# Attention scores as two half-width products of TensorE each, in place of one full-width product

## The chip, the core and the metric

The kernel runs on one core of a Trainium2 chip. The engines of the core that matter here are TensorE (PE in the profile; its weight loads are listed apart, as PEld), VectorE (DVE), ScalarE (ACT), GpSimd (POOL) and SyncE (SP), which issues most of the DMAs. The metric is the device time of one execution, in microseconds; lower is better. All values are fp32.

## The reference

The program is a "macaron" layer on x of 8 batches x 1024 tokens x 256 features: half a mixture-of-experts feed-forward, a causal attention, and another half feed-forward, each on the layer-normed x and added to it. Cut to what matters:

```
x = x + 0.5 * ffn(layernorm(x))
x = x + attn(layernorm(x))
x = x + 0.5 * ffn(layernorm(x))

attn:  q, k, v = projections, 16 heads of 16 features
       dots = (q * 16**-0.5) @ k.T          # 1024 x 1024 for each batch and head
       dots = where(j > i, -1e9, dots)      # causal
       out  = softmax(dots) @ v;  return out @ Wo.T + bo
ffn:   top-2 routing over 8 experts; an expert's tokens count only if they
       are at most 1280 (counts <= cap), otherwise the whole expert is left out
```

With these inputs every expert is asked for more than its capacity, so both feed-forwards add nothing. The kernel computes the routing counts and branches over the feed-forward; the trace shows no load of expert weights. What runs is the attention and the routing.

## The kernel before, in words

The attention works in 32 units: 8 batches x 4 groups of 4 heads (`u`, `b`, `g`). For a unit, qT and kT hold its 4 heads on 128 partitions, 32 for each head: 16 features, and one row that carries a correction. On the key side that row is -1, on the query side it is first 0 and later the row maximum, so that the second score product comes out with its maximum already subtracted.

Each head's scores are computed twice. `m_steps` (`block`, L862) computes them with queries on the partitions (tiles named sm): VectorE takes the row maximum from them, with the causal mask added on the diagonal block. `settle` (L893) carries the maxima through DRAM into qT. `e_steps` (`scores`, L910) computes them with keys on the partitions (tiles named sc): ScalarE writes their exponential to pT in SBUF, GpSimd zeroes the upper triangle of the diagonal block, and `values` (L934) multiplies pT by v (tile pav), with a column of ones beside v that gives the row sums.

A score product has 32 rows of contraction (a head's partitions), 128 stationary columns and 128 to 512 moving columns. The head decides the 32 partitions, and so the row group of the 128 x 128 array; four heads use the four row groups. The other large products (pav; pv, pq and px, the projections) go through `matmul_cols` (L714): 128 rows of contraction by 32 stationary columns, four of them on the four column groups.

A unit has 24 steps. In the main loop (L1241) a step issues, for h = 0 and 1, one sc product of unit u and one sm product of unit u + 1: four products on four row groups, in the order sc, sm, sc, sm. After them come the pav products of an earlier step (two steps later for the first half of the columns, three for the second), and a piece of other work (`Beside.step`, L79: projections of coming units, layer norms, output projection, routing). The wrapper `InOrder` (L27) keeps the instructions of TensorE, VectorE, ScalarE and GpSimd in the order written.

Score products write to six PSUM banks that are handed out in turn (`score`, L695); the other two banks (`bank`, L699) serve everything else. A step asks for four score banks, so its first two products use those of the second head of two steps before, and its last two those of the first head of the step before. A bank is free once ScalarE (sc) or VectorE (sm) has read it.

Of the kernel before, what the change touches and what calls it, by code (L numbers as in the profile page):

```python
# [18 lines left out]
P = 128  # L19
# [81 lines left out]
def macaron_kernel(  # L101
# [78 lines left out]
    for k in range(4):  # L180
        gpsimd.affine_select(
            out=row16,
# [498 lines left out]
    def attention(run_no, src, dst, gate0, logits, tally):  # L681
# [3 lines left out]
        with stack:  # L685
# [9 lines left out]
            def score(name):  # L695
                asked[0] += 1
                return ps_score.tile([P, 512], F32, tag=f"score{asked[0] % 6}", name=name)

            def bank(name):  # L699
                return ps_bank.tile([P, 512], F32, tag="bank", name=name)  # L700
# [5 lines left out]
            def matmul(out, lhsT, rhs, start=True, stop=True):  # L706
                pe.matmul(out, lhsT=lhsT, rhs=rhs, start=start, stop=stop)
# [6 lines left out]
            def matmul_cols(out, lhsT, rhs, start=True, stop=True):  # L714
                for r in range(0, P, 32):
                    matmul(out[r : r + 32], lhsT[:, r : r + 32], rhs, start, stop)

            xbs, xnTs, lns, stds, att_ds, gate_lns, lgs = {}, {}, {}, {}, {}, {}, {}


# [138 lines left out]
            def m_steps(u):  # L859
                qT, kT = qTs[u % 4], kTs[u % 4]  # L860

                def block(ib, j0, pr, h):  # L862
                    hf, i = divmod(ib, 4)
                    w = min(512, (ib + 1) * P - j0)
                    r = 64 * pr + 32 * h
                    sc = score(f"sm{u}_{ib}_{pr}_{j0}_{h}")
                    matmul(sc[:, :w], qT[r : r + 32, ib * P : (ib + 1) * P], kT[r : r + 32, j0 : j0 + w])
                    if j0 + w < (ib + 1) * P:
                        so_far = first[ib, r] = ap.tile([P, 1], F32, tag="first", name=f"first{u}_{ib}_{r}", bufs=18)
                        vector.tensor_reduce(so_far, sc[:, :w], AX.X, ALU.max)  # L870
                    else:

                        vector.tensor_tensor_reduce(
                            out=sc[:, :w],
                            in0=sc[:, :w],
                            in1=causal[:, 512 - w :],
                            scale=1.0,
                            scalar=first.pop((ib, r), LOWEST),
                            op0=ALU.add,
                            op1=ALU.max,  # L880
                            accum_out=tops[hf][:, r // 8 + i : r // 8 + i + 1],
                        )

                first = {}
                todo = [(ib, 0) for ib in (3, 2, 1, 0)]
                todo += [(ib, 0) for ib in (4, 5, 6, 7)] + [(ib, 512) for ib in (7, 6, 5, 4)]
                for ib, j0 in todo:
                    for pr in range(2):
                        yield lambda h, ib=ib, j0=j0, pr=pr: block(ib, j0, pr, h)
# [15 lines left out]
            def e_steps(u):  # L905
                b, g = divmod(u, NG)
                qT, kT = qTs[u % 4], kTs[u % 4]
                pav = {}

                def scores(hf, jb, pr, out, h):  # L910
                    off = max(0, jb - 4 * hf) * P
                    w = 512 - off
                    r = 64 * pr + 32 * h
                    sc = score(f"sc{u}_{hf}_{jb}_{pr}_{h}")
                    matmul(sc[:, :w], kT[r : r + 32, jb * P : (jb + 1) * P], qT[r : r + 32, hf * 512 + off : hf * 512 + 512])
                    if h == 0:
                        out[pr] = ap.tile([P, 2, 512], F32, tag="pT", name=f"pT{u}_{hf}_{jb}_{pr}", bufs=8)
                    pT = out[pr]
                    scalar.activation(pT[:, h, :w], sc[:, :w], AF.Exp)
                    if h == 0:  # L920
                        return
                    if jb >= 4 * hf:
                        gpsimd.affine_select(
                            out=pT[:, :, :P],
                            in_=pT[:, :, :P],
                            pattern=[[0, 2], [1, P]],
                            compare_op=ALU.is_ge,
                            fill=0.0,
                            base=0,
                            channel_multiplier=-1,  # L930
                        )


                def values(hf, jb, pTs, part):  # L934
                    if jb == 0 and part == 0:
                        pav[hf] = bank(f"pav{u}_{hf}")
                    off = max(0, jb - 4 * hf) * P
                    w = 512 - off
                    if w <= 256:
                        cols = slice(0, w)  # L940
                        if part == 1:
                            return
                    else:
                        cols = slice(part * w // 2, (part + 1) * w // 2)
                    for pr in (1, 0):
                        for h in range(2):
                            r = 64 * pr + 32 * h
                            v0 = (4 * g + 2 * pr + h) * VW
                            matmul(
                                pav[hf][r : r + 32, off + cols.start : off + cols.stop],  # L950
                                vaugs[b % 2][:, jb, v0 : v0 + 32],
                                pTs[pr][:, h, cols],
                                start=(jb == 0 and part == 0),
                                stop=(jb == 4 * hf + 3),
                            )
                    if u == NU - 1 and jb == 4 * hf + 3:
                        if part == 0:
                            last.append(pav.pop(hf))
                    elif jb == 4 * hf + 3 and part == 0:
                        att = ap.tile([P, 512], F32, tag="att", name=f"att{u}_{hf}", bufs=4)  # L960
                        scalar.copy(att, pav.pop(hf))
                        if g == 0:
                            att_ds[b, hf] = spill.tile(
                                [NH, 32, 512], F32, tag="att_d", name=f"att_d{run_no}_{b}_{hf}", bufs=3
                            )
                        nc.sync.dma_start(
                            out=att_ds[b, hf][4 * g : 4 * g + 4].rearrange("h r c -> (h r) c"), in_=att
                        )

                for hf in range(2):  # L970
                    for jb in range(4 * hf + 4):
                        pTs = {}
                        yield (lambda h, hf=hf, jb=jb, pTs=pTs: scores(hf, jb, 1, pTs, h)), None
                        yield (
                            (lambda h, hf=hf, jb=jb, pTs=pTs: scores(hf, jb, 0, pTs, h)),
                            (lambda part, hf=hf, jb=jb, pTs=pTs: values(hf, jb, pTs, part)),
                        )
# [319 lines left out]
    logits = [route.tile([P, NT, E], F32, name=f"logits{k}") for k in range(2)]  # L1297
    tallies = [tally_tile("0"), tally_tile("1")]
    leasts = attention(0, x, out, (logits[0], tallies[0]), logits[1], tallies[1])
    some0 = kept("0", leasts[0])  # L1300
    either = route.tile([P, 1], I32, name="either")
    vector.scalar_tensor_tensor(either, leasts[1], float(CAP), some0, ALU.is_le, ALU.max)
    with tc.If(branch_on(either) > 0):
        some1 = kept("1", leasts[1])

        with tc.If(flag(some0, "0") > 0):
            feed_forward(0, logits[0], x, xw_d)
            tally = tally_tile("1b")
            anew = attention(1, xw_d, out, None, logits[1], tally)
            vector.tensor_copy(some1, kept("1b", anew[1]))  # L1310
        with tc.If(flag(some1, "1") > 0):
            feed_forward(1, logits[1], out, out)
# [40 lines left out]
```

## Time and profile before

| what | value |
|---|---|
| time before, median of 3 runs | 1412.6 us (1409.44 to 1412.75) |
| the profiled execution: its time, its span | 1412.56 us, 1410.7 us |
| PE busy, share of the span | 1373.3 us, 97% |
| PE weight loads busy | 526.3 us, 37% |
| DVE, ACT, POOL busy | 73%, 56%, 28% |
| mean granted TensorE clock | 0.983 |
| sm product records | x3072, 537 ns in the mean |
| sc product records | x3072, 534 ns in the mean |
| pav product records | x5120, 370 ns in the mean |

An fp32 product stands in the profile as two records of a weight load (LDWEIGHTS) and two of a product (MATMUL), so 3072 records are 1536 products of the program. A form such as `32*128 32x512` reads: 32 active rows by 128 active columns of the array, moving operand 32 partitions x 512 columns. Records of TensorE overlap and their ends are modelled, so differences of starts tell more than durations. Nearly every operation of the attention is issued from one helper line (L37), so the names of the tiles tell the instructions apart. `x8` on a timeline row is a run of eight merged records. The busy time counts an engine as busy as long as any record of it is open.

### The profile page before, as it was taken

Reading aid. Unit: us, or ns where it says so; the run is one execution under the profiler, and the core shown is the slowest. Engines: PE = TensorE matmul, PEld = TensorE weight load, DVE = VectorE, ACT = ScalarE, POOL = GpSimd, SP = SyncE. Lnnn points to the kernel's source line nnn. Section 1 sums busy time; section 2 is a strip of 40 time slices with the busy share of each in tenths; the row PEclk is TensorE's granted clock in tenths of the full one; section 3 lists DMA queues with packets and bytes.
Section 4 is the critical chain, followed back from the end, with each engine's and each line's share of the span. In section 5 each row is a group of like instructions: output and inputs, shape, how many; then the busy total and the mean of one; then the engine's idle time right before and its main releaser. Section 6 shows DMA issues by size and latency. Waiting matters only on the chain.

```text
span 1410.7 us, 37948 instructions
## 1 busy us (share of the span) xinstructions
PE 1373.3 (97%) x14520; PEld 526.3 (37%) x14520; DVE 1032.9 (73%) x3417; ACT 788.5 (56%) x1790; POOL 399.0 (28%) x720
## 2 busy tenths in 40 slices
PE   7999999999999999999999999999999999999994
PEld 3334333343433333343333433334333333334431
DVE  4757677876778868777677777787677786778854
ACT  3246555555655656555555556555665565655561
POOL 3015114241143412352131421424114331222221
PEclk9889999999999999999999999999999999999997
DMA  4010101212111210212112121122111111121100
GB/s 146 10 40 26 41 25 50 57 61 72 34 54 60 73 44 29 78 49 71 40 35 70 43 87 32 48 65 69 52 32 58 55 47 41 42 65 63 42 26 33
DMA packets 66966, 72.85 MB, mean 52 GB/s; under 512 B 24688, under 2 KB 42232, under 8 KB 66776
## 3 DMA queue, kind: packets, MB, share of 16 engines
q1 hardware_dynamic: 65688, 69.82, 16.4%
q8 instruction: 116, 1.90, 0.5%
q14 instruction: 74, 0.61, 0.1%
q10 hardware_dynamic: 1088, 0.53, 0.1%
HBM read 26.87 MB, written 26.20 MB: 38 GB/s over the span
## 4 chain that ended last, share of the span: by engine, by line
PE 93%; DVE 3%; POOL 2%; issue 1%; DMA 0%; ACT 0%; ACTq 0%; POOLq 0%
PE sc L37 43%; PE pav L37 23%; PE pq L37 8%; PE sm L37 8%; PE pv L37 4%; PE px L37 4%; PE pta L37 1%; DVE sm L37 1%; POOL rstd_a L37 1%; POOL xa L37 1%; DVE first L37 0%; DMA bqT<-in_L_attn_bq_dram 0%; POOL pT L37 0%; PE px_last L37 0%; PE pg L37 0%
## 5 line engine op out<-in xcount | busy, mean ns | idle before, releaser
L37 ACT ACTIVATE pT<-sc 128x512 f32<-128x512 f32 (+3 forms) x1536 | 668.9, 488 | 533.3 <-PE sm L37 437.9
L37 PE MATMUL sm<-kT,qT 32*128 32x512 f32 (+3 forms) x3072 | 786.1, 537 | 0.2
L37 PE MATMUL sc<-qT,kT 32*128 32x512 f32 (+3 forms) x3072 | 735.2, 534 | 0.3 <-ACT pT L37 0.3
L37 POOL TENSOR_SCALAR_AFFINE_SELECT pT<-pT 128x256 f32<-128x256 f32 x512 | 208.0, 409 | 943.7 <-ACT pT L37 940.7
L37 DVE TENSOR_REDUCE first<-sm 128x1 f32<-128x512 f32 x512 | 328.5, 684 | 145.9 <-PE sm L37 143.9
L37 PEld LDWEIGHTS sc<-qT,kT 32*128 32x128 f32 x3072 | 258.2, 183 | 352.0 <-ACT pT L37 267.1
L37 PE MATMUL pav<-pT,vaug 128*32 128x256 f32 (+2 forms) x5120 | 386.2, 370 | 2.9 <-POOL pT L37 2.8
L37 DVE CUSTOM_DVE_ANT_0 sm<-sm,causal,first 128x256 f32<-128x256 f32 (+3 forms) x512 | 262.4, 556 | 80.1 <-PE sm L37 72.0
L37 PEld LDWEIGHTS sm<-kT,qT 32*128 32x128 f32 x3072 | 297.4, 184 | 22.7 <-DVE top L37 8.6
L37 DVE CUSTOM_DVE_ANT_0 sm<-sm,causal 128x256 f32<-128x256 f32 (+3 forms) x512 | 241.7, 515 | 85.6 <-PE sm L37 68.9
L37 PEld LDWEIGHTS pav<-pT,vaug 128*32 128x32 f32 x5120 | 103.7, 108 | 333.2 <-issue 219.1
L37 DVE DVE_READ_ACCUMULATOR2_ANT top<- 128x1 f32 x1024 | 145.2, 142 | 0.0
L37 PE MATMUL pv<-wvT,xnT 128*32 128x264 f32 x1024 | 83.7, 400 | 0.0
L37 PE MATMUL px<-woT,on 128*32 128x264 f32 x960 | 76.1, 389 | 0.0
L37 PE MATMUL pq<-xnT,wkT 128*32 128x512 f32 x512 | 68.4, 610 | 1.4 <-ACT xnT L37 1.4
L37 POOL TENSOR_SCALAR xn_a<-xa,mv_a,rstd_a 128x256 f32<-128x256 f32 x56 | 67.9, 1224 | 1.9 <-PE pta L37 1.0
L37 PE MATMUL pq<-xnT,wqT 128*32 128x512 f32 x512 | 67.4, 601 | 0.0
L37 POOL TENSOR_TENSOR on<-on,inv 128x512 f32<-128x512 f32 (+1 forms) x32 | 40.9, 1277 | 13.7 <-DMA inv<-inv_d 13.7
L37 PEld LDWEIGHTS pv<-wvT,xnT 128*32 128x32 f32 x1024 | 29.0, 111 | 41.5 <-issue 23.4
L37 POOL TENSOR_TENSOR xa<-xa,bo_all 128x528 f32<-128x528 f32 x32 | 41.8, 1306 | 0.6
L37 PEld LDWEIGHTS px<-woT,on 128*32 128x32 f32 x960 | 27.9, 109 | 33.5 <-issue 10.6
L37 ACT COPY vaug<-pv 128x256 f32<-128x256 f32 x64 | 24.4, 381 | 26.2 <-PE pv L37 25.2
(126 smaller groups left out, 482.6 us busy)
## 6 DMA issues: line engine op xcount, KB each, us to landing
att_d<-att SPq DMA_DIRECT2D x62, 256.0 KB
kT<-packed SPq DMA_DIRECT2D x256, 32.0 KB
qT<-packed SPq DMA_DIRECT2D x256, 32.0 KB
out_dram<-xa SPq DMA_DIRECT2D x16, 512.0 KB
on<-att_d SPq DMA_DIRECT2D x30, 256.0 KB
inv<-inv_d SPq DMA_DIRECT2D x30, 256.0 KB
xa<-in_L_attn_x_dram SPq DMA_DIRECT2D x7, 1024.0 KB
xa<-in_L_attn_x_dram SPq DMA_DIRECT2D x2, 512.0 KB
```

Of the source, the lines that this page charges most:

```text
L37: i = call(*args, **kwargs)
```

## The change

Both score products go through a new helper, which cuts the stationary operand and the output into two halves of 64 columns (64 output partitions). Each half is a product of its own: 32 rows by 64 columns, with the same moving operand and the same PSUM bank. Four products of a step become eight. Nothing else is changed.

```diff
+            def matmul_tiles(out, lhsT, rhs):
+                for r in range(0, P, 64):
+                    matmul(out[r : r + 64], lhsT[:, r : r + 64], rhs)
+
@@ block, of m_steps
-                    matmul(sc[:, :w], qT[r : r + 32, ib * P : (ib + 1) * P], kT[r : r + 32, j0 : j0 + w])
+                    matmul_tiles(sc[:, :w], qT[r : r + 32, ib * P : (ib + 1) * P], kT[r : r + 32, j0 : j0 + w])
@@ scores, of e_steps
-                    matmul(sc[:, :w], kT[r : r + 32, jb * P : (jb + 1) * P], qT[r : r + 32, hf * 512 + off : hf * 512 + 512])
+                    matmul_tiles(sc[:, :w], kT[r : r + 32, jb * P : (jb + 1) * P], qT[r : r + 32, hf * 512 + off : hf * 512 + 512])
```

## The prediction

> **What bounds the kernel now.** I read the chain of waits first, to see which engine ends last and on which products.
>
> ```profile
> PE 93%; DVE 3%; POOL 2%; issue 1%; DMA 0%; ACT 0%; ACTq 0%; POOLq 0%
> PE sc L37 43%; PE pav L37 23%; PE pq L37 8%; PE sm L37 8%; PE pv L37 4%; PE px L37 4%; PE pta L37 1%; DVE sm L37 1%; POOL rstd_a L37 1%; POOL xa L37 1%; DVE first L37 0%; DMA bqT<-in_L_attn_bq_dram 0%; POOL pT L37 0%; PE px_last L37 0%; PE pg L37 0%
> ```
>
> TensorE is the chain for 93% of the span, and the two score products that the diff touches, sc and sm, hold 51% of it. A busy TensorE need not be a full one, so I went on to its timeline in one stretch (start, duration, what), where every score product shows as two records (an fp32 product is run as two weight loads and two passes).
>
> ```profile
> 706.92 0.69 PE L37 MATMUL sc<-qT,kT 32*128 32x512 f32 x1
> 706.92 0.69 PE L37 MATMUL sm<-kT,qT 32*128 32x512 f32 x1
> 706.93 0.69 PE L37 MATMUL sc<-qT,kT 32*128 32x512 f32 x1
> 706.94 0.69 PE L37 MATMUL sm<-kT,qT 32*128 32x512 f32 x1
> 707.45 0.59 PE L37 MATMUL sc<-qT,kT 32*128 32x512 f32 x1
> ...
> 707.47 0.59 PE L37 MATMUL sm<-kT,qT 32*128 32x512 f32 x1
> 707.99 0.65 PE L37 MATMUL pv<-wvT,xnT 128*32 128x264 f32 x8
> 708.57 0.69 PE L37 MATMUL sc<-qT,kT 32*128 32x512 f32 x1
> 708.58 0.69 PE L37 MATMUL sm<-kT,qT 32*128 32x512 f32 x1
> 708.78 0.69 PE L37 MATMUL sc<-qT,kT 32*128 32x512 f32 x1
> 708.89 0.67 PE L37 MATMUL sm<-kT,qT 32*128 32x512 f32 x1
> ...
> 709.40 0.59 PE L37 MATMUL sm<-kT,qT 32*128 32x512 f32 x1
> 709.91 0.42 PE L37 MATMUL pav<-pT,vaug 128*32 128x128 f32 x8
> ...
> 711.25 0.59 PE L37 MATMUL sc<-qT,kT 32*128 32x512 f32 x1
> ...
> 711.68 0.59 PE L37 MATMUL sc<-qT,kT 32*128 32x512 f32 x1
> ```
>
> Two things are to be seen. First, a group of four products after a product of the other shape: the four first passes start within 0.02 us, the second passes 0.53 us later, the next shape 0.52 us after the last of those. But at 711.25, where scores follow scores, the next pass comes after 0.43 us, which is the pure pass (512 columns, 0.833 ns each, 427 ns). So the first pass of a group pays 0.53 - 0.43 = about 107 ns ahead of it, and the end of the group 0.52 - 0.43 = about 90 ns. The 107 ns is the weight load, seen only behind a change of shape; later loads hide under the pass before. Second, the group at 708.57 has its second head late, by 0.21 us (sc) and 0.31 us (sm). The timeline of the engines that empty the banks says why:
>
> ```profile
> 708.12 1.29 DVE L37 TENSOR_REDUCE first<-sm 128x1 f32<-128x512 f32 x2 [1.03 <-PE sm L37]
> 708.13 1.08 ACT L37 ACTIVATE pT<-sc 128x512 f32<-128x512 f32 x2 [1.20 <-PE sm L37]
> ```
>
> The first of the two exponentials ends at 708.13 + 0.54 = 708.67, the first maximum at about 708.77: six score banks, four taken by each group, so a group's second head needs the banks of the first head before it. The loads by shape:
>
> ```profile
> L37 PEld LDWEIGHTS sm<-kT,qT 32*128 32x128 f32 x3072 | 297.4, 184 | 22.7 <-DVE top L37 8.6 <-issue 4.0 <-DVE first L37 3.4
> L37 PEld LDWEIGHTS sc<-qT,kT 32*128 32x128 f32 x3072 | 258.2, 183 | 352.0 <-ACT pT L37 267.1 <-issue 82.7 <-DVE turned L37 0.8
> L37 PEld LDWEIGHTS pav<-pT,vaug 128*32 128x32 f32 x5120 | 103.7, 108 | 333.2 <-issue 219.1 <-POOL pT L37 67.9 <-PE sc L37 22.0
> ```
>
> 184 ns for 128 columns and 108 for 32: 76 ns for 96 columns, about 0.8 ns a column, so about 51 ns less for 64 columns fewer. That fits the 107 ns seen for 128.
>
> To weigh both, I took the starts of all PE records from the trace, cut them into groups wherever the shape changes, and let each pass last 0.833 ns a column. There are 738 groups of scores. From their last pass to the next shape 90 to 91 ns go by in the typical case, and 96 ns from the other shapes to the scores, with hardly any spread: neither switch waits for anything but TensorE. Beyond its passes a group takes 126 to 127 ns in 431 cases (20 ns from first to fourth start, plus the load); 307 groups take more, because a head is late. Passes of the scores make 491.5 us, their excess 192 us.
>
> [...] 90 to 96 ns at each switch, none at 711.25; and the change leaves the number of switches alone. [...] the trace shows 6.7 (0.02 us for four), and I use that.
>
> **The change part by part.** Each of the 3072 score products becomes two, of 64 weight columns each, with the same moving rows and the same bank, on its upper and lower 64 partitions.
>
> *Passes.* Nothing: a half streams the same N columns, and both halves of a row group run at once if eight tiles do. The case before that resembles it is the 128x32 shape: four tiles that share all rows and write four parts of one bank, and x8 records of 264 columns take 0.58 us (707.99 to 708.57): two passes of 220 ns, a 27 ns load, 20 ns of starts, 95 ns of switch make 582. So tiles of different columns do load and stream together.
>
> *Load.* 107 to 53 ns: -54 ns for each group behind a switch.
>
> *Starts.* Eight tiles start over 7 x 6.7 = 47 ns where four took 20: +27 ns at the group's end. So an undelayed group saves 127 - 100 = 27 ns: 431 x 27 = 11.6 us.
>
> *Late groups.* The wait of a second head runs from the first head's products through one exponential or maximum. Those products end 47 ns (sc) and 40 ns (sm) earlier, but the group in front also ends 27 earlier, so the wait seen shrinks by 13 to 20; the late head's own load saves 54 less 7 for its second half, 47. That is 60 to 67 ns for a late group behind one on time, 47 where late ones follow each other (one loop, one load and one start), 27 if the wait vanishes. It needs ACT or DVE to have been idle before that instruction. Following each late start back to its releaser, that holds for 36 of 66 us of lateness; the rest stands behind a busy VectorE (statistics, small routing work), and gains maybe 0 to 27. I take 55% x 50 + 45% x 15 = 34 ns: 307 x 34 = 10.5 us.
>
> *Waits, queues, buffers.* The first half carries the waits for bank and DMA, the second finds them met; what is queued behind a waiting half is what was queued before. Semaphores go up after the second half. ACT, DVE, POOL and SP keep their instructions and order; VectorE at 73% becomes about 74%. 6144 more loads and 6144 more passes are to be fetched: PE goes from 29040 instructions to 41328. The page's queue q8 moves 1.90 MB in 116 packets in the whole run, 0.5% of the DMA time; half as much again I cost at nothing[...] a packet would cost up to its own DMA time, 0.5% x 16 x 1410.7 / 116 = 1 us, and some 50 more packets 50 us; nothing in the trace shows PE waiting for one.
>
> Sum: -11.6 - 10.5 = -22.1 us. The profiled execution took 1412.56 us (span 1410.7, 1.9 us around it), which is the median of the runs, 1412.6; so 1390.5 us.
>
> The price not seen before is that of eight tiles together. Bounds: if starts cost nothing more, 738 x 54 = 40 us less (1372.6). If the halves of one row group load in turn, the load stays 107 and the starts still spread: 738 x 27 = 20 us more. I take the middle value, since load and starts are both seen for tiles of rows and for tiles of columns, only not together.
>
> **Rivals.** *The emptying engines take half of it back*: late groups gain nothing, as VectorE's pace sets them; 1412.6 - 11.6 = 1401. For it: VectorE is busy 74 to 79% of three stretches of 100 us in mid-run and most late starts wait for it. Against it: 36 of 66 us of lateness begin with that engine idle. *More than forecast*: starts of two halves fall together, or lateness shrinks further; 1372. Against it: the 128x32 groups show 6.7 ns between column tiles too. *Loads of the two halves of a row group in turn*, the one that ends slower: at every group's head, +27 ns, 1412.6 + 20 = 1433. It decides once load and starts exceed today's 127 ns, which also happens if starts are over (127 - 53) / 7 = 10.6 ns apart. Against it: four column tiles load in 27 ns on the same rows. *Nothing moves*: the halves behave as the whole, with load and starts just trading; 1412. For it only that the two terms, 54 and 27, are close.
>
> **How the numbers follow.** Forecast 1390.5 (1382 to 1398): 0.55. Half given back, 1401: 0.18. More, 1372: 0.12. Nothing: 0.05. Slower, 1433: 0.10. The range leaves out the slower case and the edges of the fast one: 1370 to 1408. A measurement of this kernel tells about 0.3%, 4.2 us, from no change: faster 0.85, same 0.05, slower 0.10.
>
> **What would show it.** In the profile after: score rows of form 32*64, 6144 of each kind, their loads near 130 ns; eight starts within about 0.05 us; second passes about 0.48 us after the first in a 512 group behind a switch (0.53 now); group to next shape about 1.04 us (1.07 now); switches still 90 to 96 ns. The forecast is wrong if second passes still come at 0.53 us (loads in turn), if eight starts spread beyond 0.08 us, if passes stretch beyond 0.43 us where scores follow scores (halves not at once: up to 491.5 us more, which the 128x32 shape speaks against), or if the saved time reappears as later second heads, with more idle time of PE loads until DVE top.

## The result, and the profile after

The changed kernel takes 1393.5 us in the median of four runs (1393.18 to 1394.04), against 1412.6 us before (1409.44 to 1412.75): a ratio of 0.9868, 95% interval 0.9854 to 0.9883. That is 19.0 us less, where 22.1 were forecast (1390.5 us). The span went from 1410.7 to 1391.5 us, at the same mean granted TensorE clock, 0.983.

The chain of waits of the changed kernel is still TensorE's, with the scores' share down from 51% to 49%:

```profile
PE 91%; DVE 4%; POOL 2%; issue 1%; SPq 1%; DMA 1%; ACT 0%; ACTq 0%; DVEq 0%; POOLq 0%
PE sc L37 40%; PE pav L37 23%; PE sm L37 9%; PE pq L37 8%; PE pv L37 4%; PE px L37 4%; PE pta L37 1%; DVE sm L37 1%; POOL rstd_a L37 1%; POOL xa L37 1%; DVE first L37 0%; DMA bqT<-in_L_attn_bq_dram 0%; SPq L862 0%; POOL pT L37 0%; SPq L856 0%
```

The same two groups as before the change, in the timeline of TensorE (start and duration in us; a row of x2 now holds one pass of the two halves of a product):

```profile
697.19 0.65 PE L37 MATMUL sc<-qT,kT 32*64 32x512 f32 x2
697.21 0.64 PE L37 MATMUL sm<-kT,qT 32*64 32x512 f32 x2
697.22 0.65 PE L37 MATMUL sc<-qT,kT 32*64 32x512 f32 x2
697.23 0.65 PE L37 MATMUL sm<-kT,qT 32*64 32x512 f32 x2
697.67 0.59 PE L37 MATMUL sc<-qT,kT 32*64 32x512 f32 x2
...
697.71 0.59 PE L37 MATMUL sm<-kT,qT 32*64 32x512 f32 x2
698.24 0.65 PE L37 MATMUL pv<-wvT,xnT 128*32 128x264 f32 x8
698.82 0.65 PE L37 MATMUL sc<-qT,kT 32*64 32x512 f32 x2
698.83 0.65 PE L37 MATMUL sm<-kT,qT 32*64 32x512 f32 x2
699.03 0.64 PE L37 MATMUL sc<-qT,kT 32*64 32x512 f32 x2
699.14 0.64 PE L37 MATMUL sm<-kT,qT 32*64 32x512 f32 x2
```

Second passes come 0.48 us after the first, where they came after 0.53: the load ahead of the pass of 427 ns is 53 ns in place of 107. Products follow each other by 0.013 us, twice the 6.7 ns of before. From the first score to the next shape it is 1.05 us (1.07 before). The second group has its second head at 0.21 (sc) and 0.32 us (sm) after its start, as before. The loads by shape:

```profile
L37 PEld LDWEIGHTS sm<-kT,qT 32*64 32x64 f32 x6144 | 213.9, 130 | 29.7 <-DVE top L37 14.4 <-issue 6.2 <-DVE first L37 3.5
L37 PEld LDWEIGHTS sc<-qT,kT 32*64 32x64 f32 x6144 | 188.5, 130 | 355.5 <-ACT pT L37 256.3 <-issue 97.4 <-DVE top L37 1.0
```

130 ns in the mean, as forecast; the DVE entry among the idle times of sm has risen from 8.6 to 14.4 us. And the engines that empty the banks of the first group:

```profile
698.37 1.08 ACT L37 ACTIVATE pT<-sc 128x512 f32<-128x512 f32 x2 [1.17 <-PE sm L37]
698.37 1.29 DVE L37 TENSOR_REDUCE first<-sm 128x1 f32<-128x512 f32 x2 [1.01 <-PE sm L37]
```

Both start 1.18 us after the group (697.19). Before, it was 1.21 for ACT and 1.20 for DVE. They gained 0.03 and 0.02 us, not the 0.047 and 0.040 by which the passes they wait for end earlier. The prediction did not have this.

Cut into groups as in the prediction, the trace says where the time came from. The stretches of scores sum to 663.6 us (683.8 before: -20.2); those of the other shapes with 32 columns to 516.5 (515.8); the switches are still 90 to 91 and 96 ns. An undelayed group takes 99 to 100 ns beyond its passes, 126 to 127 before. Of 736 groups that can be set against each other, the 430 undelayed ones of before gained 10.8 us in sum, the 306 late ones (a head of the group had to wait for its bank) 9.1 us.

### The profile page after: what moved, and what is told of

It is laid out like the page before. It is cut to its first block, busy times and chain, and to the rows that moved or that the text cites. A ratio compares the mean times of both kernels' runs of the same rounds, so it can differ in the third digit from the quotient of the medians.

```text
span 1391.5 us, 51072 instructions
## 1 busy us (share of the span) xinstructions
PE 1352.3 (97%) x20664; PEld 456.6 (33%) x20664; DVE 1029.7 (74%) x3417; ACT 788.0 (57%) x1790; POOL 399.0 (29%) x720
## 3 DMA queue, kind: packets, MB, share of 16 engines
q1 hardware_dynamic: 65688, 69.82, 16.5%
q8 instruction: 164, 2.69, 0.8%
## 4 chain that ended last, share of the span: by engine, by line
PE 91%; DVE 4%; POOL 2%; issue 1%; SPq 1%; DMA 1%; ACT 0%; ACTq 0%; DVEq 0%; POOLq 0%
PE sc L37 40%; PE pav L37 23%; PE sm L37 9%; PE pq L37 8%; PE pv L37 4%; PE px L37 4%; PE pta L37 1%; DVE sm L37 1%; POOL rstd_a L37 1%; POOL xa L37 1%; DVE first L37 0%; DMA bqT<-in_L_attn_bq_dram 0%; SPq L862 0%; POOL pT L37 0%; SPq L856 0%
## 5 line engine op out<-in xcount | busy, mean ns | idle before, releaser
L37 PE MATMUL sm<-kT,qT 32*64 32x512 f32 (+3 forms) x6144 | 759.8, 511 | 1.5 <-DMA qT<-packed 0.4
L37 PE MATMUL sc<-qT,kT 32*64 32x512 f32 (+3 forms) x6144 | 709.2, 508 | 0.0
L37 PEld LDWEIGHTS sc<-qT,kT 32*64 32x64 f32 x6144 | 188.5, 130 | 355.5 <-ACT pT L37 256.3
L37 PEld LDWEIGHTS sm<-kT,qT 32*64 32x64 f32 x6144 | 213.9, 130 | 29.7 <-DVE top L37 14.4
```

What stands on the lines that cost most here:

```text
L37: i = call(*args, **kwargs)
```

## The experiments

The theory to be tested: behind a change of shape, a group of scores pays one exposed load (its columns at 0.83 ns, as 107 ns for 128 in the trace of before) and the time to send its products one after another; halving the columns trades 54 ns of load for 27 ns of sending. The rivals: only the load counts; or the gain is one of finer pieces, which start and end sooner and feed the other engines.

**Quarters.** Sixteen tiles of 32 columns.

```diff
-                for r in range(0, P, 64):
-                    matmul(out[r : r + 64], lhsT[:, r : r + 64], rhs)
+                for r in range(0, P, 32):
+                    matmul(out[r : r + 32], lhsT[:, r : r + 32], rhs)
```

> Each score product as four of 32 rows by 32 columns, sixteen at once. Load-and-starts theory (a group of scores behind a change of shape takes load of its columns at 0.83 ns each plus 6.7 ns for each further tile, plus passes): 27 + 15 x 6.7 = 127 ns, exactly what four tiles of 128 columns take (107 + 20), so undelayed groups are as long as before the change; the completion signals, 29.5 ns for each part, reach VectorE later. 1405 to 1425 us. Rival, only the load counts and starts overlap: 738 x 80 ns = 59 us less than before, about 1354. Rival, finer is better because the emptying engines start earlier: below 1393.

Measured: 1414.0 us, ratio to the kernel before 1.0033 (1.0018 to 1.0049). All of the gain is gone. Timeline of TensorE in that run (a row of x4 holds one pass of the four parts of a product):

```profile
711.01 0.63 PE L37 MATMUL sc<-qT,kT 32*32 32x512 f32 x4
711.03 0.63 PE L37 MATMUL sm<-kT,qT 32*32 32x512 f32 x4
711.06 0.63 PE L37 MATMUL sc<-qT,kT 32*32 32x512 f32 x4
711.09 0.66 PE L37 MATMUL sm<-kT,qT 32*32 32x512 f32 x4
711.46 0.61 PE L37 MATMUL sc<-qT,kT 32*32 32x512 f32 x4
```

Second passes come after 0.45 us, so the load is 27 ns; but products of four parts start 0.027 us apart. The load and the spacing are as the theory has them, and both rivals fall. The forecast for the whole group was not met: the parts of the last product often start later than 6.7 ns each, so that the sixteenth part starts 131 ns after the first in the median undelayed group, not 100, and a typical undelayed group takes 155 ns beyond its passes, not 127. Why the last product is late was not settled. The groups that were undelayed before lost some 13 us by this, and the late ones of before gained 13 us; the stretches of scores sum to 684.4 us (683.8 before). What the kernel is slower by lies in the stretches of the other shapes, 520.0 us against 515.8.

**The moving side split.** Nearly as many products as after the change, made from the kernel before, but each with all 128 columns of weights. Both score products go through this helper; products of under 256 moving columns stay whole.

```diff
+            def matmul_spans(out, lhsT, rhs, w):
+                n = w // 2 if w >= 256 else w
+                for o in range(0, w, n):
+                    matmul(out[:, o : o + n], lhsT, rhs[:, o : o + n])
```

> From the kernel before: products of 256 to 512 moving columns cut into two of half the moving columns, with all 128 weight columns; as many products as after the change for these sizes, but four tiles and the full load. Load-and-starts theory: the load of 107 ns still shows once behind each change of shape and the others hide under passes of 107 ns or more, so as before: 1408 to 1422 us. Rival, the gain comes from more and smaller products in flight: near 1393.

Measured: 1422.3 us, ratio 1.0091 (1.0071 to 1.0111): more products in flight give no gain. Its timeline, an undelayed group of 256 columns (spans of 128) and the next shape:

```profile
709.82 0.37 PE L37 MATMUL sc<-qT,kT 32*128 32x128 f32 x1
709.83 0.37 PE L37 MATMUL sm<-kT,qT 32*128 32x128 f32 x1
709.84 0.37 PE L37 MATMUL sc<-qT,kT 32*128 32x128 f32 x1
709.86 0.37 PE L37 MATMUL sm<-kT,qT 32*128 32x128 f32 x1
710.03 0.27 PE L37 MATMUL sc<-qT,kT 32*128 32x128 f32 x1
...
710.49 0.53 PE L37 MATMUL pav<-pT,vaug 128*32 128x192 f32 x8
```

The load is again 107 ns (710.03 - 709.82 = 0.21, of which 107 ns are a pass of 128 columns). The four tiles start 0.013 us apart, not 0.007, though each waits for nothing: in the program the second span of the same tile stands between. So what costs 6.7 ns here is each product sent, whether its tile can start or not. Undelayed groups of split products take 152 ns beyond their passes (127 before): about 25 ns more for each, which is the larger part of the 12.8 us lost.

**Only sc halved.**

```diff
@@ block, of m_steps
-                    matmul_tiles(sc[:, :w], qT[r : r + 32, ib * P : (ib + 1) * P], kT[r : r + 32, j0 : j0 + w])
+                    matmul(sc[:, :w], qT[r : r + 32, ib * P : (ib + 1) * P], kT[r : r + 32, j0 : j0 + w])
```

> Only the sc products are halved, the sm products keep 128 columns; they alternate on TensorE. If every change of tile shape drains the array (32x64 against 32x128 too), no two kinds of products run together: four lone products in each group, passes of the scores four times as long in sum (491.5 to 1966 us) plus four loads and switches of some 170 ns for 738 groups (0.5 ms): about 3000 to 3300 us. Rival, only a change between 32-row and 128-row shapes drains: between 1393 and 1413.

Measured: 5643.9 us (one run), four times the time. In its timeline no product of one kind runs beside the other:

```profile
2799.07 1.97 PE L37 MATMUL sc<-qT,kT 32*64 32x512 f32 x4
2800.98 2.07 PE L37 MATMUL sm<-kT,qT 32*128 32x512 f32 x2
2802.98 1.97 PE L37 MATMUL sc<-qT,kT 32*64 32x512 f32 x4
```

A product starts every 1.9 to 2.0 us. So 32x64 against 32x128 is a change of shape here like that between scores and the other products, and the change had to be made to both products or to neither. The time is far above the 3000 to 3300 us expected, and a stretch of 1 ms of its profile shows the main reason; the third value from the end is the granted clock:

```profile
core 0: us, PE busy (x) PEld busy (x) DVE busy (x) ACT busy (x) POOL busy (x), PEclk, DMA share, GB/s
1000.00:2000.00 1000.00, 1000.00 (x3020) 255.95 (x3022) 192.71 (x561) 154.14 (x306) 69.36 (x115) 0.50 0.04 13
```

The clock was granted at half (0.511 in the mean of the run). The records of sm with 512 and with 384 columns last 1115 and 904 ns in the mean in this run, so the 128 columns between them take 1.65 ns each; in the kernel before it is 646 and 539 ns, 0.84 ns each. By an estimate from this, a product of 512 columns takes two passes of some 850 ns here, and load and switch make up the rest of the 1.9 to 2.0 us. TensorE shows 100% busy in this stretch. What lowers the clock was not tested.

**More waits of ScalarE for itself.** The engines wait for one another's semaphores in this program, and the trace has the times at which these go up. After the change 256 of the 1536 exponentials wait for ScalarE's own semaphore beside TensorE's (some 30 before). Where ScalarE stands idle before it, an exponential with two waits starts 82 to 83 ns after TensorE's signal, one with a single wait about 23. To see whether that eats into the gain I multiplied these waits:

```diff
+            kept_pTs = [fixed.tile([P, 2, 512], F32, name=f"pT{run_no}_{k}") for k in range(8)]
...
+            def next_pT():
+                turn_pT[0] += 1
+                return kept_pTs[turn_pT[0] % 8]
...
-                        out[pr] = ap.tile([P, 2, 512], F32, tag="pT", name=f"pT{u}_{hf}_{jb}_{pr}", bufs=8)
+                        out[pr] = next_pT()
```

> From the kernel after: the eight pT buffers are kept for good and taken in turn, in place of slots of a pool. The result of the planner is that 1012 of the 1536 exponentials wait also for ScalarE's own semaphore (256 in the kernel after, 31 before). If such a second wait delays an exponential by about 60 ns (it starts 82 ns after the signal in place of 22) and ScalarE is late for second heads in some 150 groups: 3 to 10 us slower than after, 1396 to 1404. If it costs nothing on the path: 1393.5 within 2.

Measured: 1392.0 us, ratio 0.9879 (0.9863 to 0.9896), against 0.9868 for the change. Four times as many of these waits cost nothing that can be told. But the run tests less than it was made for. Of the exponentials before which ScalarE stands idle, 675 of 711 had a second wait already in the changed kernel, most of them for GpSimd, and 704 of 710 have one here; the other waits that were added stand behind a busy ScalarE. The step that the change itself made, from 461 of 713 to 675 of 711, is not tested. That it cost anything is unlikely: in 257 of the 258 late groups of four products in the changed kernel (261 of 268 before), the head that comes last is that of sm, which waits for VectorE and not for ScalarE.

**The order of a step turned.** For each group the trace also records when TensorE's completion signals go up. In an undelayed group the four products signal 281, 324, 366 and 409 ns after the group's start (its two passes taken off) before the change, and 245, 305, 364 and 423 ns after it. The passes end 6.7 or 13 ns apart, but the signals stand 42.5 and 59 ns apart. So the first product is heard of 36 ns sooner, the second 19, the third 2, and the fourth 14 ns later. Signals seem to go up one after another, as in a queue. If VectorE's late start rests on that, VectorE's product should go first:

```diff
                     for h in range(2):
-                        scores(h)
                         if ms[k] is not None:
                             ms[k](h)
+                        scores(h)
```

> The changed kernel once more, as the mark for the next run on the same chip: ratio to before 0.986 to 0.988.

> The changed kernel with the order of a step turned to sm, sc, sm, sc, so that the product for VectorE, the slower one to give a bank back, is the first of each pair. Theory that completion signals of a group queue, 59 ns for each halved product: VectorE is told 59 ns sooner, ScalarE 59 ns later, and since most late heads wait for VectorE, late groups lose up to 40 to 59 ns where VectorE was idle: 3 to 8 us less than the changed kernel. Rival, each engine starts with the end of its own passes: the order moves these by 13 ns only, at most 2 us less.

Measured on one chip: the changed kernel 1392.6 us (0.9873, 0.9852 to 0.9893), the turned order 1385.8 us (0.982, 0.9798 to 0.9842): 6.8 us less. The engines behind a group that starts at 693.97:

```profile
693.97 0.65 PE L37 MATMUL sm<-kT,qT 32*64 32x512 f32 x2
...
695.09 1.29 DVE L37 TENSOR_REDUCE first<-sm 128x1 f32<-128x512 f32 x2 [1.01 <-PE sc L37]
695.21 1.09 ACT L37 ACTIVATE pT<-sc 128x512 f32<-128x512 f32 x2 [1.17 <-PE sc L37]
695.60 0.65 PE L37 MATMUL sm<-kT,qT 32*64 32x512 f32 x2
...
695.86 0.65 PE L37 MATMUL sc<-qT,kT 32*64 32x512 f32 x2
```

VectorE starts 1.12 us after the group in place of 1.18, ScalarE 1.24 in place of 1.18: the 59 ns between signals, not the 13 ns of the passes. The next group has its last head 0.26 us after its start (695.60 to 695.86), where the changed kernel had 0.32. This kernel is faster than both the kernel before and the changed one. The same turn on the kernel before:

> The kernel before with the order of a step turned to sm, sc, sm, sc, products whole. Its completion signals stand 42.5 ns apart, so VectorE is told 42.5 ns sooner in place of 59; if the queue of signals is what the order works through, it gains 42.5/59 of the 6.8 us that the same turn gave the halved products: 3.5 to 6.5 us less than before, ratio 0.9954 to 0.9975. Rival, the order works only with halves (two halves ahead of VectorE's product): no change within 0.1%.

Measured: 1404.3 us, ratio 0.9956 (0.9941 to 0.9970), about 6.2 us less by the ratio. The turn does not need the halves. Whether it gains less here in proportion to the signals (42.5 to 59) these runs don't tell. And with the turned order and the many waits of ScalarE for itself:

> The order sm, sc, sm, sc on halved products with pT buffers kept for good, so that 1012 in place of 256 exponentials wait for ScalarE's own semaphore too. ScalarE is now told second, with less room before the next group needs its bank; if the second wait's 60 ns are on the path there: 2 to 8 us slower than the turned order alone (1388 to 1394). If they are not: within 2 us of it.

Measured: 1386.1 us, ratio 0.9817 (0.9799 to 0.9836): as the turned order alone. Here, too, few of the exponentials before which ScalarE stands idle got a second wait by it (43 had a single one before, 7 after), so it shows no more than that waits behind a busy ScalarE cost nothing.

**Less of VectorE's lateness.** Half of the maximum's work is left out, in the kernel before and in the changed one:

```diff
-                        vector.tensor_reduce(so_far, sc[:, :w], AX.X, ALU.max)
+                        vector.tensor_reduce(so_far, sc[:, : w // 2], AX.X, ALU.max)
...
-                            out=sc[:, :w],
-                            in0=sc[:, :w],
-                            in1=causal[:, 512 - w :],
+                            out=sc[:, : w // 2],
+                            in0=sc[:, : w // 2],
+                            in1=causal[:, 512 - w : 512 - w + w // 2],
```

> The kernel before, with the row maximum taken over the first half of each block's columns only (half the work of VectorE on scores is left out), so that late heads that wait for VectorE go. All theories: some 30 to 60 us less than before; it is the mark for the next run.

> The changed kernel with the same half of the maximum's work left out. Load-and-starts theory: the change is worth 27 ns for each of 738 groups whether heads are late or not, so 17 to 22 us less than the half-maximum kernel of before. Rival, the change works through what it gives VectorE (earlier products, fewer late heads): without late heads the difference falls below 12 us. Rival, VectorE takes part of the gain back: the difference rises above 24 us.

Measured: 1373.9 us (0.9738, 0.9715 to 0.9761) and 1351.6 us (0.9586, 0.9564 to 0.9608). The change is worth 22.2 us here, just above the 17 to 22 us that the theory gave, and 17.4 us on the same chip with VectorE's whole work (1410.0 to 1392.6). Late heads are fewer in the half-maximum kernel of before, not gone: 235 groups of 738, and the lateness of heads that wait for VectorE, in groups of four products, falls from 56 to 20 us. So the gain doesn't grow smaller as VectorE's lateness does; if anything VectorE takes some of the gain back. The times alone hardly tell, since their intervals overlap, but the traces point the same way: the late groups gain 43 ns each by the change here, against 30 with the whole maximum.

## Why the prediction was right, point by point

*Load and starts of undelayed groups*: right in mechanism and size. A load of 53 ns and starts over 47 ns were forecast, and the 0.48 us and the 99 to 100 ns show them; the sum is 10.8 us against 11.6. The loads of all three widths, 107, 53 and 27 ns, are 0.83 to 0.84 ns for a column. The quarters show the other side of the trade.

*Passes, switches, fetching of instructions*: right. Halves run at once (a second pass 0.48 us after the first leaves room for one pass of 427 ns, not for two), and switches stayed at 90 to 96 ns. Queue q8, which the page lists as that of instructions, rose from 1.90 to 2.69 MB and from 116 to 164 packets; the 50 us that this could have cost by the prediction's estimate are ruled out, since all but about 1 us of the result is accounted for below.

*Late groups*: the sign was right, the step was not. It said that a late head's wait shrinks by 13 to 20 ns, since the products ahead end 47 and 40 ns earlier. But the engines start on signals that go up 42.5 ns apart before and 59 ns apart after the change: ScalarE started 36 and VectorE 19 ns sooner (364 to 328 and 347 to 328 ns after the group's start, passes taken off), and as the group in front ended 27 ns sooner, ScalarE's wait shrank by 9 and VectorE's grew by 8. It is VectorE's that counts, since its head comes last in nearly every late group. The sign of being wrong that the prediction named came in part: late heads start no sooner in their group (71 us of lateness in sum, counted from the group's start, against 66; an estimated 5 to 6 us of it is the regular start of the last product, 20 ns later in some 300 groups), and weight loads stood idle until VectorE's maximum for 14.4 us, against 8.6. What was left, by this sum, is the late head's own load: 47 - 8 = 39 ns. Late groups behind one on time gained these 39 ns in the mean (60 to 67 forecast). Late ones behind late ones gained 17.5 (47 forecast); why is not settled, though in the half-maximum kernels such groups gain 58 ns, which points to VectorE's pace. The mean of both is 30, and the term is 9.1 us against 10.5. That the 34 taken came so near is luck in part: both kinds were forecast too high, and the discount for a busy VectorE made up for it. The trace of the kernel before already had its signals 42.5 ns apart, and the prediction did not use it. Between the signals of products in one, two and four parts there are 42.5, 59 and 92.5 ns (kernel before, change, quarters), by which each further part adds 16.5 to 16.8 ns.

*The rest*: 10.8 + 9.1 = 19.9 of the 22.1 us; the scores' stretches give 20.2, and about 1 us of it is lost in the other stretches and the ends (the span fell by 19.3).

*The rivals*: half given back by the emptying engines (1401) is the direction in which the result lies from the forecast, by some 30% of that way (3 of 10.5 us) and in the main for another reason, the signals. Loads in turn (1433) fell at the first second pass, 0.48 us. Nothing moves (1412) and more than forecast (1372) fell with the time; the ground given for the first, that the two terms are close, did not hold from the start, as 54 is twice 27.

## What to carry to other kernels

Behind each change of tile shape TensorE paid a switch (90 to 96 ns each way), one weight load and the sending of the products in these runs, and only the last two depended on how the array is cut: with 4, 8 and 16 tiles the load was 107, 53 and 27 ns, and the starts of the group spread over 20, 47 and 131 ns, so that eight was the best of the three. Products that are to run at once should all have the same shape: mixing 32x64 and 32x128 cost a factor of four here (5643.9 us, at half the clock). Of several products that go out together, try first in order the one whose reader is slowest to give the bank back; their completions were signalled 42.5 or 59 ns apart, and the order alone was worth 6 to 7 us with whole and with halved products.

## What the runs showed of the hardware that was not expected

- Completion signals of products that end 7 to 27 ns apart go up 42.5 ns apart for whole products (kernel before), 59 ns for products in two halves or two spans (one signal for both), and 92.5 ns for four quarters.
- A product that had to wait for its own tile still delayed the product behind it by 6.7 ns (starts 13 ns apart with split moving operands, 6.7 with whole ones).
- An exponential that waited for two semaphores started 82 to 83 ns after TensorE's signal, one that waited for TensorE alone 23 ns after it (before and after the change, ScalarE idle).
- With one score product at a time, on 32 rows of the array, TensorE was granted half its clock (0.50 in mid-run, 0.511 in the mean, against 0.983 before), although its records show it 100% busy in that mid-run millisecond.
